# A selective scan in 128 steps: four state tiles and four decay tiles instead of five and three, and the experts' choice spread over the steps

## The chip, the cores and the metric

The kernel runs on one core of a Trainium2 chip. The time is the device time of one execution in microseconds (us). A core has five engines, each with its own queue that it works through in order: TensorE (PE in the profile; PEld are its weight loads), VectorE (DVE), ScalarE (ACT), GpSimd (POOL) and SyncE (SP), which here issues most of the DMA transfers. [...]

## What is computed

Two transformer layers on x of 4 x 256 tokens by 512. Layer 0 is an attention with low-rank latents beside a gated feed-forward; layer 1 is a Mamba block beside a mixture of LoRA experts. The part that matters here is layer 1:

```python
proj = hidden_states @ in_proj_w            # x, z = split; 1024 channels each
xc = silu(conv4(x) + conv_b)                # causal, 4 taps, per channel
ssm_p = einsum('bdl,ed->ble', xc, x_proj_w) # 32 for dt, 16 for B, 16 for C
dt_r, Bm, Cm = rmsnorm of the three parts
dt = softplus(dt_r @ dt_proj_w.T + dt_bias)
# for every t:  h = exp(dt*A)*h + dt*B*x ;  y = sum over 16 states of h*C
y = (ys + D_param * xc) * silu(z)
out = y @ out_proj_w.T
...
logits = x @ router_W.T                     # 8 experts
probs = softmax(logits); top 2, lowest index first on a tie
rw = top_vals / sum(top_vals)
inc = ((x @ lora_A) * w_dense) @ lora_B     # 16 ranks an expert
x = x + mamba + x @ base_W.T + inc * 2
```

## The kernel before, in words

Everything is laid out by hand: the order in the program is the order in each engine's queue. Layer 0 and the convolution of the first batch take the time up to about 327 us. Then come `total` = 128 steps, one for each batch b (4), block of 128 channels c (8) and group of four states g (4), so `u = 32*b + 4*c + g`; `PER` is 32 and `NU` 4. A tile of a step is 128 partitions by 4 x 256: 32 channels times four states on the partitions, four channel quarters and 256 tokens along the row.

One step u goes through the engines like this:

- `spread` (L937): SP copies `dt` and `dt*x` of a block c, which POOL made and `send` (L933) wrote to device memory, into the tiles `dts` and `dus` (two buffers each), four DMAs each.
- `decays` (L971): ACT makes `exp(dt*A)` in four activations, into one of the `decay` tiles. There are three, `decay[(u-4) % 3]`, and the loop calls `decays(u + 2)` at the start of step u, so ACT can be two steps ahead.
- `scan_in` (L986): DVE multiplies B (`brow`, in PSUM) and `dus` into `bx`, a tile in PSUM with one buffer. From step 8 on a no-op of DVE's stands in front of it and waits for what the scan will need: the decays of u, and `hc` of step u-2.
- `scan` (L998): one DVE instruction runs the recurrence along the row, `h <- decay, bx`; POOL multiplies `h` with C into a tile of its own, `hc`. `h` has two buffers, `hc` three. The first four steps use tiles that belong to others (`lent`, L961).
- `states_sum` (L1019): eight PE instructions add up the states of `hc` into `ysum` (PSUM, one buffer). Step u's sum is the last PE work of step u+1.
- `take_sum` (L1028) on ACT, `gate` (L1032) on POOL, `out_mm` (L1120) and `out_x` (L1124) make the output.

Between these stands the rest of the work, put at a step by hand: `put(b, s, f, ...)` (L1248) places a call at the start of step 32b+s, `put_mid` between `bx` and the scan, `put_late` behind the scan, `put_end` behind the sum. Within a step the order is: `take_sum`, `decays`, what `put` placed, `scan_in`, what `put_mid` placed, `scan`, `gate`, what `put_late` placed, `states_sum` of the step before, what `put_end` placed.

During a batch the next one is prepared: `norm_stats` to `norm_copy` (L718 to L748), `px_mm` (L754), `conv_in`, `conv_taps` (L765, L793), `conv_silu` (L821), then `pp_mm` (L829; the first half at the end of step 17, the second at 18), `pp_square` (L836, at 19: ACT `sq`, a PE product, ACT `rs` twice), `pp_norm` (L844, DVE `nrm`, between `bx` and scan of step 21), `step_in` (L865; PE, then ACT; 21 and 22), `step_exp` (L880, ACT, two halves at 23), `step_out` (L912, POOL, 24 to 29), `step_x` (L923). `pz_mm` (L945) and `gate_silu` (L953) make the gate; the latter loads another activation table and loads the old one back. Products that leave PE go through `psmm`, three buffers in PSUM for all of them.

The experts are chosen in batches 0 and 2, for two batches at once. `router` (L1039) makes logits and LoRA products of 128 tokens, PE then an ACT copy into one part of the tile `ml`; the four stand at steps 16, 17, 19 and 20. `route_exp` (L1066) stands at step 23: two DVE operations on 128 x 32 and the exponential on ACT. `route` (L1072) stands at step 25 ahead of `bx`: 16 small DVE operations in a row on a tile `w` that takes the place of `bx` in PSUM, and four products `mid` on 128 x 128. `expert_turn` (L1098), `dense` (L1108) and `expert_out` (L1115) use the result on PE.

Of the kernel before, what the change touches and what calls it, by code (L numbers as in the profile page):

```python
# [41 lines left out]
def block_kernel(  # L42
# [894 lines left out]
    def spread(n, b, c):  # L937
        t = w1.tile([P, NG, S], F32, tag=f"{n}s", name=f"{n}s", bufs=2)
        src = live[n, b, c // 2][c % 2].rearrange("(k j) t -> j k t", k=NG)
        for i in range(NG):  # L940
            nc.sync.dma_start(t[i * NB : (i + 1) * NB], src)
        live[n + "s", b, c] = t
# [10 lines left out]
    def gate_silu(b, *ps):  # L953
# [6 lines left out]

    lent = {  # L961
        "d": ("d", "w_in", "d", "w_in"), "h": ("w_in", "u", "e", "u"),
        "hc": ("w_in", "lw", "w_in", "lw"),
    }

# [5 lines left out]
    def decays(u):  # L971
        b, c, g = u // PER, u % PER // NU, u % NU
        if u >= len(lent["d"]):
            da = decay[(u - 4) % 3]
        elif lent["d"][u] == "d":
            da = decay[0]
        else:
            da = lend("d", u)
            nc.gpsimd.memset(da[:, :, 0:1], 0.0)
        live["da", u] = da  # L980
        for k in range(NG):
            made["da", u] = nc.scalar.activation(  # L982
                da[:, k, 1:], live["dts", b, c][:, k, 1:], AF.Exp, scale=aneg[:, c, k, g : g + 1]
            )

    def scan_in(u):  # L986
        b, c, g = u // PER, u % PER // NU, u % NU
        if u >= 8:
            i = nc.vector.engine_nop()
            for n in (("da", u), ("hc", u - 2)):  # L990
                tc.add_manual_dep(i.ins, made[n].ins.name, early, reason="the scan's waits")
        bx = psx.tile([P, NG, S], F32, tag="bx", name="bx")
        nc.vector.tensor_tensor(  # L993
            bx, brow[g // 2][:, g % 2, :].unsqueeze(1).to_broadcast([P, NG, S]), live["dus", b, c], ALU.mult
        )
        live["bx"] = bx

    def scan(u, parts=1):  # L998
        b, c, g = u // PER, u % PER // NU, u % NU
        da, bx = live.pop(("da", u)), live["bx"]  # L1000
        if u < len(lent["h"]):
            h, hc = lend("h", u), lend("hc", u)
        else:
            h = act.tile([P, NG, S], F32, tag="h", name="h", bufs=2)
            hc = act.tile([P, NG, S], F32, tag="hc", name="hc", bufs=3)
        for k in range(parts):
            n = slice(k * NG // parts, (k + 1) * NG // parts)
            nc.vector.tensor_tensor_scan(  # L1008
                h[:, n].rearrange("p n t -> p (n t)"), da[:, n].rearrange("p n t -> p (n t)"),
                bx[:, n].rearrange("p n t -> p (n t)"), 0.0, ALU.mult, ALU.add,  # L1010
            )

            made["hc", u] = (nc.vector if k == NG - 1 else nc.gpsimd).tensor_tensor(  # L1013
                hc[:, n], h[:, n],
                crows[b][:, g, :].unsqueeze(1).to_broadcast([P, NG // parts, S]), ALU.mult,
            )
        live["hc", u] = hc

    def states_sum(u):  # L1019
# [4 lines left out]
        for k in range(NG):  # L1024
            mm(ysum[k * NB : (k + 1) * NB, :], lhsT=stack, rhs=hc[:, k, :],  # L1025
               start=False, stop=(g == NU - 1))

# [20 lines left out]
    NR = 4  # L1048
    m1 = w1.tile([P, NR], F32, name="m1")
    b2 = w1.tile([P, NR], F32, name="b2")  # L1050
    ex = w1.tile([P, NR, NE], F32, name="ex")
    sel2 = w1.tile([P, NR, NE], F32, name="sel2")
    rev = cst[:, C_REV : C_REV + NE].unsqueeze(1).to_broadcast([P, NR, NE])
# [3 lines left out]

    def first_of(out, tmp, val, top):

        nc.vector.tensor_reduce(top, val, AX.X, ALU.max)  # L1060
        nc.vector.tensor_tensor(tmp, val, over(top), ALU.is_equal)
        nc.vector.tensor_tensor(tmp, tmp, rev, ALU.mult)
        nc.vector.tensor_reduce(m1, tmp, AX.X, ALU.max)
        nc.vector.tensor_tensor(out, tmp, over(m1), ALU.is_equal)

    def route_exp(b):  # L1066
        lg = live["ml"][:, :, 0:NE]
        nc.vector.tensor_reduce(m1, lg, AX.X, ALU.max)
        nc.vector.tensor_tensor(ex, lg, over(m1), ALU.subtract)
        nc.scalar.activation(ex, ex, AF.Exp)  # L1070

    def route(b):  # L1072

        w = psx.tile([P, NG, S], F32, tag="bx", name="w")
        m2 = w[:, 0, 0:NR]
        sel, best, tmp = (
            w[:, k, 0 : NR * NE].rearrange("p (i e) -> p i e", e=NE) for k in (1, 2, 3)
        )
        first_of(sel, sel, ex, m2)

        nc.vector.scalar_tensor_tensor(best, sel, -4.0, ex, ALU.mult, ALU.add)
        first_of(sel2, tmp, best, b2)
        nc.vector.tensor_tensor(sel, sel, sel2, ALU.add)
        nc.vector.tensor_tensor(sel, sel, ex, ALU.mult)
        nc.vector.tensor_tensor(m2, m2, b2, ALU.add)
        nc.vector.reciprocal(b2, m2)

        nc.vector.scalar_tensor_tensor(sel, sel, 2.0, over(b2), ALU.mult, ALU.mult)
        for n in range(2):
            mid = act.tile([P, 2, NE, LR], F32, tag="mid", name="mid", bufs=2)  # L1090
            for i in (2 * n, 2 * n + 1):
                nc.vector.tensor_tensor(
                    mid[:, i % 2], live["ml"][:, i, NE:].rearrange("p (e r) -> p e r", r=LR),
                    sel[:, i, :].unsqueeze(2).to_broadcast([P, NE, LR]), ALU.mult,
                )
            live["mid", b + n] = mid

# [129 lines left out]
    def open_act():  # L1227
        nonlocal act
        l0.close()
        act = ctx.enter_context(tc.tile_pool(name="act", bufs=1))  # L1230
        decay_tile(act)
        decay_tile(act)
        for n, shape, d in (("rl", [P, HC, NE + P], rl_d), ("bw", [P, HC, D], base_d),
# [29 lines left out]
    for b in range(B):  # L1263
# [59 lines left out]
        if nxt < B:  # L1323
# [21 lines left out]
            put(b, 22, c_rows, nxt, 0)  # L1345
            if b % 2 == 0:
                put(b, 23, route_exp, b)
            put(b, 23, step_exp, nxt, 0, slice(0, 2))
# [12 lines left out]
            put(b, 25, load_z, nxt, 1)  # L1361
            for k, u in enumerate((27, 28, 29, 31)):
                put(b, u, pz_mm, nxt, k // 2, k % 2)
            if b % 2 == 0:
                for i, u in enumerate((16, 17, 19, 20)):
                    put(b, u, router, b, i)
                put(b, 25, route, b)
            put(b, 26, expert_turn, b)
            put(b, 25, dense, b, 1, 0)
            put(b, 26, dense, b, 1, 1)  # L1370
            put(b, 28, expert_out, b, 1)
        else:
# [165 lines left out]
```

## Time and profile before

| | us |
|---|---|
| runs of the kernel before: median (lowest to highest, 3 runs) | 840.59 (839.35 to 841.75) |
| the profiled execution's own time | 840.18 |
| its span, from the first to the last instruction | 838.4 |
| granted TensorE clock, mean over the span | 0.953 |
| busy in the span: PE | 750.9 (90%) |
| DVE | 654.6 (78%) |
| ACT | 554.2 (66%) |
| POOL | 496.9 (59%) |
| PE busy from 345 to 832 us (487 us) | 421.7 |

Busy time is counted from an instruction's start to its end; waits, branches and the issue of DMAs are not counted. The shares are means over the whole span: DVE, at 78% in all, is busy for nine tenths and more of most slices after 430 us. A row of the groups names the line, the engine, what is written and read, how often, the busy time, the mean time of one in nanoseconds and, after the last bar, how long the engine had stood idle just before and what ended that. In a view in order of time each row has the start, the time taken, the engine and line, and in brackets the idle time before it.

### The profile page before, as it was taken

How to read it: one execution, taken by the hardware profiler on the slowest of the kernel's cores; microseconds unless marked ns; L12 is line 12 of the kernel's file. 1: busy time of each engine (PE TensorE's matmuls, PEld its weight loads, DVE VectorE, ACT ScalarE, POOL GpSimd, SP SyncE). 2: the span in 40 equal slices, each digit the busy share in tenths (PEclk: the TensorE clock that was granted, in tenths of full speed). 3: DMA queues.
4: the chain of work that ended last, by engine and by line, in shares of the span. 5: the costliest groups of instructions: out<-in, count | busy, mean ns of one | idle time of the engine just before them, and what ended most of it. 6: DMA issues, size and time to landing. Idle time of an engine off the chain costs nothing.

```text
span 838.4 us, 11286 instructions
## 1 busy us (share of the span) xinstructions
PE 750.9 (90%) x3846; PEld 429.6 (51%) x3846; DVE 654.6 (78%) x604; ACT 554.2 (66%) x1124; POOL 496.9 (59%) x389
## 2 busy tenths in 40 slices
PE   4999999999999999999887999897899987876985
PEld 2665545666555676666543456444457544322331
DVE  4486756288644535797899999988999999999996
ACT  4335564435556277699895898687898787865661
POOL 3133232001343333678878799769799769798775
PEclk9799999999999999999999899989999989988898
DMA  7233332001222322454593544433554443443400
GB/s 226 63 101 106 96 101 63 1 1 38 76 76 79 115 57 64 149 141 126 130 217 109 160 150 115 126 91 105 144 165 114 112 110 92 119 114 120 113 26 25
DMA packets 68644, 86.72 MB, mean 103 GB/s; under 512 B 12221, under 2 KB 52169, under 8 KB 68458
## 3 DMA queue, kind: packets, MB, share of 16 engines
q1 hardware_dynamic: 58794, 65.81, 29.0%
q0 software_dynamic: 9072, 18.35, 7.8%
q10 hardware_dynamic: 720, 1.84, 0.6%
q8 instruction: 30, 0.49, 0.3%
q14 instruction: 28, 0.23, 0.1%
HBM read 66.58 MB, written 10.22 MB: 92 GB/s over the span
## 4 chain that ended last, share of the span: by engine, by line
PE 45%; DVE 23%; POOL 12%; ACT 9%; issue 5%; DMA 5%; SPq 1%; POOLq 0%; ACTq 0%; DVEq 0%
DVE h L1008 11%; POOL hc L1013 8%; PE pg L444 6%; DVE bx L993 6%; PE pu L444 5%; PE po L469 5%; PE av L397 4%; ACT decay L982 3%; PE po L1121 2%; PE px L759 2%; DMA dus<-dud 2%; PE scT L386 2%; DVE mpl L354 2%; PE ysum L1025 2%; DMA dts<-dtd 2%
## 5 line engine op out<-in xcount | busy, mean ns | idle before, releaser
L1013 POOL TENSOR_TENSOR hc<-h,cr 128x1024 f32<-128x1024 f32 (+1 forms) x130 | 301.9, 2324 | 80.5 <-DVE h L1008 70.4
L1008 DVE TENSOR_TENSOR_SCAN h<-decay,bx 128x1024 f32<-128x1024 f32 (+1 forms) x129 | 288.1, 2235 | 8.5 <-PE po L469 3.6
L982 ACT ACTIVATE decay<-dts,aneg 128x255 f32<-128x255 f32 x504 | 213.6, 501 | 52.8 <-DVE h L1008 38.2
L993 DVE TENSOR_TENSOR bx<-brow,dus 128x1024 f32<-128x1024 f32 x128 | 157.7, 1232 | 24.2 <-ACT decay L982 9.3
L1025 PE MATMUL ysum<-hc,stack 128*32 128x256 f32 x1024 | 88.4, 417 | 39.3 <-POOL hc L1013 39.3
L456 POOL TENSOR_TENSOR hlo<-g,hhi 128x512 fp32r<-128x512 f32 x28 | 35.8, 1280 | 115.0 <-ACT hhi L455 115.0
L354 DVE TENSOR_REDUCE mpl<-sc 128x4 f32<-128x1024 f32 x64 | 76.7, 1220 | 22.8 <-PE sc L352 21.3
L427 POOL DMA_DIRECT2D wgu<-in_wgu x56 | 31.1, 555 | 96.0 <-PE pg L444 95.0
L388 ACT ACTIVATE pe<-scT 128x1024 f32<-128x1024 f32 x64 | 64.0, 1023 | 22.9 <-PE sc L352 14.3
L1121 PE MATMUL po<-ow,xc 128*128 128x512 f32 x128 | 72.4, 671 | 5.3 <-POOL xc L1033 4.9
L1025 PEld LDWEIGHTS ysum<-hc,stack 128*32 128x32 f32 x1024 | 21.2, 111 | 99.1 <-POOL hc L1013 69.7
L950 PE MATMUL pz<-xn1T,w_in 128*128 128x256 f32 x256 | 69.3, 419 | 0.0
L759 PE MATMUL px<-xn1T,w_in 128*128 128x256 f32 x256 | 61.0, 383 | 0.4 <-ACT sz L956 0.3
L950 PEld LDWEIGHTS pz<-xn1T,w_in 128*128 128x128 f32 x256 | 50.2, 205 | 19.8 <-issue 11.6
L759 PEld LDWEIGHTS px<-xn1T,w_in 128*128 128x128 f32 x256 | 47.5, 190 | 13.1 <-issue 3.1
L452 DVE SCALAR_TENSOR_TENSOR g<-g,pg 128x512 f32<-128x512 f32 x28 | 19.2, 687 | 43.0 <-ACT g L451 43.0
L444 PE MATMUL pg<-xhi,wgu 128*128 128x512 f32 x112 | 49.7, 443 | 1.0 <-ACT xhi L244 1.0
L469 PE MATMUL po<-wd,hhi 128*128 128x512 f32 x112 | 49.2, 439 | 0.0
L444 PE MATMUL pu<-xhi,wgu 128*128 128x512 f32 x112 | 47.5, 424 | 0.8 <-DVE g L454 0.8
L455 ACT CAST hhi<-g 128x512 fp32r<-128x512 f32 x28 | 17.3, 619 | 45.8 <-DVE g L454 45.8
L444 PE MATMUL pg<-xlo,wgu 128*128 128x512 f32 x112 | 44.9, 401 | 0.7 <-DVE xlo L251 0.7
L444 PE MATMUL pu<-xlo,wgu 128*128 128x512 f32 x112 | 44.6, 398 | 0.0
(237 smaller groups left out, 1276.8 us busy)
## 6 DMA issues: line engine op xcount, KB each, us to landing
dts<-dtd SPq DMA_DIRECT2D x124, 128.0 KB, 2.8
dus<-dud SPq DMA_DIRECT2D x124, 128.0 KB, 3.0
wgu<-in_wgu POOLq DMA_DIRECT2D x56, 256.0 KB, 2.7
w_in<-in_inz SPq DMA_DIRECT2D x16, 512.0 KB, 4.7
w_in<-in_inx SPq DMA_DIRECT2D x14, 512.0 KB, 4.4
dtd<-dt SPq DMA_DIRECT2D x15, 256.0 KB, 2.3
dud<-du SPq DMA_DIRECT2D x15, 256.0 KB, 2.3
wd<-in_wd POOLq DMA_DIRECT2D x7, 512.0 KB, 3.5
```

Source lines behind the costliest of these rows:

```text
L354: nc.vector.tensor_reduce(mpl2[b % 2][:, qb, 2 * hp : 2 * hp + 2, 16 + 2 * gq : 18 + 2 * gq], sc.rearrange("p i (f k) -> p i f k", f=2), A ...
L388: nc.scalar.activation(pes[b, k][:, 2 * t : 2 * t + 2, :], sc, AF.Exp)
L444: mm(ps, lhsT=wgus[i][:, hc, :], rhs=xs[j][:, hc, :], start=(hc == 0 and j == 0), stop=(hc == HC - 1 and j == 1))
L469: mm(po, lhsT=hids[th][j][:, m, i * P : (i + 1) * P], rhs=wd[:, m, :], start=False, stop=(m == MC - 1 and j == 1))
L759: mm(px[:, i, :], lhsT=w[:, i, hc, :], rhs=xns[b][:, hc, :], start=(hc == 0), stop=(hc == HC - 1))
L950: mm(pz[:, i, :], lhsT=w[:, i, hc, :], rhs=xns[b][:, hc, :], start=(hc == 0), stop=(hc == HC - 1))
L982: made["da", u] = nc.scalar.activation(da[:, k, 1:], live["dts", b, c][:, k, 1:], AF.Exp, scale=aneg[:, c, k, g : g + 1])
L993: nc.vector.tensor_tensor(bx, brow[g // 2][:, g % 2, :].unsqueeze(1).to_broadcast([P, NG, S]), live["dus", b, c], ALU.mult)
L1008: nc.vector.tensor_tensor_scan(h[:, n].rearrange("p n t -> p (n t)"), da[:, n].rearrange("p n t -> p (n t)"), bx[:, n].rearrange("p n t -> ...
L1013: made["hc", u] = (nc.vector if k == NG - 1 else nc.gpsimd).tensor_tensor(hc[:, n], h[:, n], crows[b][:, g, :].unsqueeze(1).to_broadcast([ ...
L1025: mm(ysum[k * NB : (k + 1) * NB, :], lhsT=stack, rhs=hc[:, k, :], start=False, stop=(g == NU - 1))
L1121: mm(live["po", b, i], lhsT=xcs[b][:, c, i * P : (i + 1) * P], rhs=late_w["ow"][:, c, :], start=False, stop=(c == DC - 1))
```

## The change

- `h` gets four buffers, and POOL multiplies with C in place; `hc` as a tile is gone (`lent` loses its third row, and step 1 takes `lw` instead of `u`).
- There are four decay tiles, and `decays(v)` is called at step v-3 (v-2 for the first step of a batch; 5 and 6 at step 3), where it was v-2.
- The no-op in front of `bx` waits for the decays of u, for the product with C of step u-4, for the sum of step u-4, and at the first step of a block for the four DMAs of `dus`.
- The choice works on the logits' difference from their maximum; only the second weight's exponential is taken (`e2`, two small activations on ACT). It is a generator of 15 DVE operations: operation 1 behind scan 20, 2 between `bx` and scan of 21, 3 behind scan 21, and so on to 15 behind scan 27. They work on tiles of their own in SBUF. The `mid` products go to POOL, one for each batch of the two, behind steps 27 and 28.
- The four `router` stand at 16, 17, 18 and 19. In batches 0 and 2, `dense`, `expert_turn` and `expert_out` stand three steps later, and one `pz_mm` at 31 instead of 29.

```diff
-        for i in range(NG):
-            nc.sync.dma_start(t[i * NB : (i + 1) * NB], src)
+        made[n, b, c] = [nc.sync.dma_start(t[i * NB : (i + 1) * NB], src) for i in range(NG)]
...
-    lent = {
-        "d": ("d", "w_in", "d", "w_in"), "h": ("w_in", "u", "e", "u"),
-        "hc": ("w_in", "lw", "w_in", "lw"),
-    }
+    lent = {"d": ("d", "w_in", "d", "w_in"), "h": ("w_in", "lw", "e", "u")}
+    ahead = 3
...
-            da = decay[(u - 4) % 3]
+            da = decay[(u - 4) % (ahead + 1)]
...
         if u >= 8:
             i = nc.vector.engine_nop()
-            for n in (("da", u), ("hc", u - 2)):
-                tc.add_manual_dep(i.ins, made[n].ins.name, early, reason="the scan's waits")
+            first = made["du", b, c] if g == 0 else []
+            for j in (*first, made["da", u], made["hc", u - 4], made["sum", u - 4]):
+                tc.add_manual_dep(i.ins, j.ins.name, early, reason="the scan's waits")
...
-            h = act.tile([P, NG, S], F32, tag="h", name="h", bufs=2)
-            hc = act.tile([P, NG, S], F32, tag="hc", name="hc", bufs=3)
+            h = act.tile([P, NG, S], F32, tag="h", name="h", bufs=4)
...
-                hc[:, n], h[:, n],
+                h[:, n], h[:, n],
...
+    def route():
+
+        vec_ = nc.vector
         lg = live["ml"][:, :, 0:NE]
+        vec_.tensor_reduce(m1, lg, AX.X, ALU.max)
+        yield
+        vec_.tensor_tensor(dl, lg, over(m1), ALU.subtract)
+        yield
+        vec_.scalar_tensor_tensor(sel1, dl, 0.0, rev, ALU.is_equal, ALU.mult)
+        yield
+        vec_.tensor_reduce(m1, sel1, AX.X, ALU.max)
+        yield
+        vec_.tensor_tensor(sel1, sel1, over(m1), ALU.is_equal)
+        yield
+
+        vec_.scalar_tensor_tensor(dl, sel1, -3e38, dl, ALU.mult, ALU.add)
+        yield
+        vec_.tensor_reduce(b2, dl, AX.X, ALU.max)
+        nc.scalar.activation(e2, b2, AF.Exp)
+        nc.scalar.activation(m1, e2, AF.Identity, bias=1.0)
+        yield
+        vec_.tensor_tensor(sel2, dl, over(b2), ALU.is_equal)
+        yield
+        vec_.tensor_tensor(sel2, sel2, rev, ALU.mult)
+        yield
+        vec_.tensor_reduce(b2, sel2, AX.X, ALU.max)
+        yield
+        vec_.tensor_tensor(sel2, sel2, over(b2), ALU.is_equal)
+        yield
+        vec_.reciprocal(m1, m1)
+        yield
+        vec_.tensor_tensor(sel2, sel2, over(e2), ALU.mult)
+        yield
+        vec_.tensor_tensor(sel1, sel1, sel2, ALU.add)
+        yield
+
+        vec_.scalar_tensor_tensor(sel1, sel1, 2.0, over(m1), ALU.mult, ALU.mult)
+        yield
+
+    def expert_mid(b, n):
+        mid = act.tile([P, 2, NE, LR], F32, tag="mid", name="mid", bufs=2)
+        i = slice(2 * n, 2 * n + 2)
+        nc.gpsimd.tensor_tensor(
+            mid, live["ml"][:, i, NE:].rearrange("p i (e r) -> p i e r", r=LR),
+            sel1[:, i, :].unsqueeze(3).to_broadcast([P, 2, NE, LR]), ALU.mult,
         )
+        live["mid", b + n] = mid
...
-            for k, u in enumerate((27, 28, 29, 31)):
+            for k, u in enumerate((27, 28, 29, 31) if b % 2 else (27, 28, 31, 31)):
                 put(b, u, pz_mm, nxt, k // 2, k % 2)
             if b % 2 == 0:
-                for i, u in enumerate((16, 17, 19, 20)):
+                for i, u in enumerate((16, 17, 18, 19)):
                     put(b, u, router, b, i)
-                put(b, 25, route, b)
-            put(b, 26, expert_turn, b)
-            put(b, 25, dense, b, 1, 0)
-            put(b, 26, dense, b, 1, 1)
-            put(b, 28, expert_out, b, 1)
+                choice = route()
+                for k in range(15):
+                    (put_late, put_mid)[k % 2](b, 20 + (k + 1) // 2, next, choice)
+                put_late(b, 27, expert_mid, b, 0)
+                put_late(b, 28, expert_mid, b, 1)
+            o = 3 if b % 2 == 0 else 0
+            put(b, 26 + o, expert_turn, b)
+            put(b, 25 + o, dense, b, 1, 0)
+            put(b, 26 + o, dense, b, 1, 1)
+            put(b, 28 + o, expert_out, b, 1)
...
+    due = {}
+    for v in range(5, total):
+        due.setdefault(max(v - ahead + (v % PER == 0), 3), []).append(v)
     for u in range(total + 2):
...
-        if 3 <= u < total - 2:
-            decays(u + 2)
+        for v in due.get(u, ()):
+            decays(v)
```

More of the change, by code (lines that the diff above doesn't have):

```diff
@@ L1001, in scan @@
         if u < len(lent["h"]):
[L1002 removed]
+            h = lend("h", u)
         else:
[L1004 to L1005 removed]
+            h = act.tile([P, NG, S], F32, tag="h", name="h", bufs=4)
         for k in range(parts):
@@ L1013, in scan @@
             made["hc", u] = (nc.vector if k == NG - 1 else nc.gpsimd).tensor_tensor(
-                hc[:, n], h[:, n],
+                h[:, n], h[:, n],
                 crows[b][:, g, :].unsqueeze(1).to_broadcast([P, NG // parts, S]), ALU.mult,
             )
-        live["hc", u] = hc
+        live["hc", u] = h
     def states_sum(u):
@@ L1024, in states_sum @@
         for k in range(NG):
-            mm(ysum[k * NB : (k + 1) * NB, :], lhsT=stack, rhs=hc[:, k, :],
-               start=False, stop=(g == NU - 1))
+            made["sum", u] = mm(ysum[k * NB : (k + 1) * NB, :], lhsT=stack, rhs=hc[:, k, :],
+                                start=False, stop=(g == NU - 1))
     def take_sum(b, c):
@@ L1048, in block_kernel @@
     NR = 4
[L1049 to L1052, printed above, removed]
+    m1, b2, e2 = (w1.tile([P, NR], F32, name=n) for n in ("m1", "b2", "e2"))
+    dl, sel1, sel2 = (w1.tile([P, NR, NE], F32, name=n) for n in ("dl", "sel1", "sel2"))
     rev = cst[:, C_REV : C_REV + NE].unsqueeze(1).to_broadcast([P, NR, NE])
@@ L1056, in over @@
         return v.unsqueeze(2).to_broadcast([P, NR, NE])
[L1058 to L1066, printed above, removed]
-        lg = live["ml"][:, :, 0:NE]
-        nc.vector.tensor_reduce(m1, lg, AX.X, ALU.max)
-        nc.vector.tensor_tensor(ex, lg, over(m1), ALU.subtract)
-        nc.scalar.activation(ex, ex, AF.Exp)
@@ L1072, in route @@
[L1072 to L1077, printed above, removed]
-        )
[L1079 to L1096, printed above, removed]
+    def route():
+        vec_ = nc.vector
+        lg = live["ml"][:, :, 0:NE]
+        vec_.tensor_reduce(m1, lg, AX.X, ALU.max)
[30 more added lines that the diff above has]
+        yield
@@ L1230, in open_act @@
         act = ctx.enter_context(tc.tile_pool(name="act", bufs=1))
-        decay_tile(act)
-        decay_tile(act)
+        for _ in range(ahead):
+            decay_tile(act)
         for n, shape, d in (("rl", [P, HC, NE + P], rl_d), ("bw", [P, HC, D], base_d),
@@ L1345, in block_kernel @@
             put(b, 22, c_rows, nxt, 0)
-            if b % 2 == 0:
-                put(b, 23, route_exp, b)
             put(b, 23, step_exp, nxt, 0, slice(0, 2))
```

## The prediction

> **What bounds the kernel now.** I read the groups first, then who waited for whom, then the order in time of DVE, ACT and PE around each wait. Up to 327 us the feed-forward and attention stages run, which the change doesn't touch. From 327 to 830 us come 128 steps: step u is the u-th `bx` and the u-th `h` (counted from 0), batch b is steps 32b to 32b+31.
>
> ```profile
> L1008 DVE TENSOR_TENSOR_SCAN h<-decay,bx 128x1024 f32<-128x1024 f32 (+1 forms) x129 | 288.1, 2235 | 8.5 <-PE po L469 3.6
> L982 ACT ACTIVATE decay<-dts,aneg 128x255 f32<-128x255 f32 x504 | 213.6, 501 | 52.8 <-DVE h L1008 38.2
> L993 DVE TENSOR_TENSOR bx<-brow,dus 128x1024 f32<-128x1024 f32 x128 | 157.7, 1232 | 24.2 <-ACT decay L982 9.3
> ```
>
> An undisturbed step starts its scan 1.27 us after its `bx`, and the next `bx` 2.32 us after that: 3.59 us, DVE's own work. 128 of them are 460 of the 503 us; the rest is small work and waits. The waits of `bx` are these (the view of line 993):
>
> ```profile
>   ACT decay L982: 9.3, 8
>   POOL hc L1013: 6.7, 10
>   ACT pad L771: 3.2, 1
> ```
>
> The 3.2 us (step 16) I count to POOL: `hc` of step 14 ended 0.2 us before that `bx`. So 19 us are what four tiles can remove at most. But DVE isn't alone. In each batch PE and ACT make the next batch's convolution, then `pp`, `sq`, `rs`, and DVE's `nrm` (step 21) needs `rs`. From 349.9 to 403 us ACT has 0.2 us of idle time, and from 362 to 408 PE has 1.8, all of it waiting for ACT: a wait that DVE loses there comes back at the end of that chain. This is ACT at that end, in batch 0 (start, length, line):
>
> ```profile
> 413.59 0.27 ACT L1046 COPY ml<-pr 128x136 f32<-128x136 f32 x1
> 413.76 3.29 ACT L982 ACTIVATE decay<-dts,aneg 128x255 f32<-128x255 f32 x8
> 417.25 0.38 ACT L839 ACTIVATE sq<-pp 64x256 f32<-64x256 f32 x1 [0.20 <-PE pp L833]
> 418.39 0.47 ACT L714 ACTIVATE rs<-pp,eps 64x256 f32<-64x256 f32 x1 [0.76 <-PE pp L840]
> 418.89 0.42 ACT L715 ACTIVATE rs<-rs 64x256 f32<-64x256 f32 x1
> 419.51 0.27 ACT L1046 COPY ml<-pr 128x136 f32<-128x136 f32 x1 [0.21 <-PE pr L1044]
> ```
>
> ACT fills the wait for `pp` with two steps' decays, and `ml` comes after `rs`.
>
> **The parts.** *State tiles.* `bx` waits for `hc` of step u-4 instead of u-2; that ended 7.2 us or more before every `bx`, so all ten waits on POOL go. Late next is `ysum` of step u-4 (PE), which DVE now waits for itself: it ended 0.64 us before `bx` at step 53, 1.6 at 21, 1.8 at 57, 2.2 at 85, over 2.7 elsewhere. Multiplying in place costs POOL nothing (L918, in place, 1.27 us; L927, not in place, 1.27). The extra wait of the no-op is checked under the 2.29 us scan: steps with one and with more semaphore checks both take 3.59. I take 0; were a 0.05 us check exposed at each, 6 us.
>
> *Decay tiles.* ACT computes each step's decays one step (3.59 us) earlier; its gate, the scan that frees the tile, is the same number of instructions back. Where ACT has idle time ahead of a burst, the lead is real; where it has none, everything behind comes 1.6 us later. The largest wait, step 58:
>
> ```profile
> 557.23 1.70 ACT L982 ACTIVATE decay<-dts,aneg 128x255 f32<-128x255 f32 x4
> ...
> 565.33 1.70 ACT L982 ACTIVATE decay<-dts,aneg 128x255 f32<-128x255 f32 x4
> ...
> 567.16 1.23 DVE L993 TENSOR_TENSOR bx<-brow,dus 128x1024 f32<-128x1024 f32 x1 [4.12 <-ACT decay L982]
> ```
>
> Between the two groups lie eight activations of `step_exp`. The second slot now makes step 59, whose `bx` stood at 570.75.
>
> *The choice.* Removed from DVE: at step 25 `bx` started at 438.80 instead of 434.17, at 89 5.36 us late (0.83 of it a wait for `ex`), and 0.2 at each `route_exp`: 10.4 in all. Added: 15 small operations, each alone, twice. The trace has neighbours: `sh` (0.13 us) ahead of a `bx` delayed it 0.07; `nrm` (0.47) between `bx` and scan delayed that 0.26; in the old chain each operation took 0.23. Nearest to a lone 0.2 us operation are the first two: 0.1, with 0.05 and 0.23 as ends: 3.0 us (1.5 to 6.9). Four `mid` products go to POOL as two (0.72 each by the 128x256 row of L1033): POOL then lags some 3 us at steps 27 to 31, covered by the four tiles; without that cover DVE would wait the 3 us.
>
> [...]
>
> *The new waits of the choice.* They are what I weigh most. `router` 2 moves from step 19 to 18, behind the second half of `pp` on PE, and its `ml` copy stands on ACT ahead of the decays of step 22 and of `sq`. `sq` thus waits for `router` and a decay group, and the first of the 15 (after scan 20) reads all four `ml`, the last of which is behind `rs`. Behind it on DVE stand `bx` 21, `nrm` and everything later.
>
> **The sum, by batch** (against the trace).
> Batch 0: decays 5, 6 and 7 now precede the table load at 353.18; no idle time absorbs it: +1.5 along the chain (bounds 0, 1.7), `pp` ends 417.2 + 1.5 = 418.7. Then `router` 1.2, copy 0.3, decays 1.7, `sq` 0.4, its product 0.7, `rs` 0.95 (`router` 3 runs beside it), `ml` 0.3, hand-overs 0.3: 424.5; `bx` 21 at 424.7, not 419.38: +5.3. All that DVE saved up to there (8.6) is lost in this wait. Steps 21 to 25 took 19.42; now 4 x 3.59 + 0.27 + 8 x 0.1 = 15.4: -4.0. Six more operations +0.6, the `hc` wait of step 29 -0.8. Together +1.1.
> Batch 1: `dense`, `expert_turn`, `expert_out` and one `pz` of batch 0 move to steps 28 to 31, 4.4 us more PE work in 14; PE's 6 us of idle there take most of it, but step 31 has 6 us, so `step_in` comes 1.3 late, of which 0.8 is absorbed at 507 (PE waited for `hc`). `bx` 59 follows its decays: 567.03 + 0.13 + 0.5 = 567.7, not 570.75: -3.1. The `hc` wait of step 61: -0.8. Together -3.9 (bounds -5.1, -0.8).
> Batch 2: `pp` ended 665.7; the same row of `router` to `ml` gives `bx` 85 at 671.4, not 668.50: +2.9. Steps 85 to 89: 20.15 becomes 15.4: -4.7. The tenth operation (between `bx` and scan 89) overwrites `b2`, which ACT's `e2` reads, and `e2` stands behind `step_exp`, by the rows of 681 to 690 at 690.0; DVE is there at 688.1: +1.9 (bounds 0, 4). In batch 0 this wait just misses (440.9 against 441.3). Six operations +0.6, `hc` at 93 -0.8. Together -0.1.
> Batch 3: the wait at 102 and trifles -0.5.
> Other parts at 0: the early lent tiles (`u` is free after `ysum` 3 at 354.3, wanted at 359.4; if not, ACT stands until then), the third memset (0.1).
> In all -3.4: span 838.4 - 3.4 = 835.0, with the 1.8 around it (840.18 - 838.4) 836.8. The runs shown have a median 0.4 above the profiled one, so **837** for the median.
>
> **Rivals.** *A: the chain's end doesn't hold DVE* (`ml` is there in time). For it: in the trace `ml` 3 came at 421.5, DVE read it at 426.7. Then only `rs` holds: batch 0 +0.4 -4.0 +0.6 -0.8 = -3.8, batch 2 -0.7 -4.7 +0.6 -0.8 = -5.6, batches 1 and 3 as above: 840.2 - 13.8, about 827. Against it: the order of the queues.
> *B, slower: PE's clock falls in the new wait.* Place: from `pp` to `ml` 3 PE has only `router`, `ysum`, a product and `router`, with 1.7 us pauses. Before, after 3.9 us of idle, the 16 `pp` took 5.35 where batch 2's took 3.9, and the stretch 405 to 420 has a granted clock of 0.89. If those four (1.2 + 0.65 + 0.65 + 1.2) take double, each choice costs 3.7 more: 844. It decides from some 2.7 us each. Against it: the row for 656 to 690 stayed at 0.90 through similar pauses.
> *C: it doesn't do what it says.* ACT's lead is gone at step 59 because PE's moved work makes `step_in` late by all the 3.1 us: 840, no change. For it: PE is 90% busy; against it: its idle time at 445 to 466.
>
> **Chances.** Forecast 0.48, A 0.22, B 0.18, C 0.12. Measurement tells 0.3% (2.5 us) from no change. The forecast's own range, 834 to 840, splits 0.28 faster, 0.19 same, 0.01 slower; A is faster; B slower; C 0.10 same, 0.02 slower. So 0.50, 0.29, 0.21. Range 828 to 844: B's time, and A's nearer part.
>
> **What would show it.** DVE idle 8 to 11 us after scan 20 and 3 to 5 after scan 84, ended by ACT's `ml`; `sq` behind a decay group; some 2 us ahead of the tenth operation in batch 2; no wait of `bx` on `hc`; the 4.1 us wait at step 58 under 1; steps with one small operation at 3.6 to 3.8. I am wrong if `bx` 21 comes before 422 us, if small operations cost over 0.2 each, or if waits on `ysum` add up to over 2 us.

## The result and the profile after

The changed kernel takes **846.52 us** (median of 6 runs, 845.34 to 848.07) against 840.66 for the kernel before (6 runs, 839.35 to 842.55): ratio 1.0066, 95% interval 1.0051 to 1.0081. The forecast was 837 with a range of 828 to 844, so it was wrong in sign, and the time lies outside the range. The profiled execution took 848.07 us, span 846.1.

These are the three large groups of the page of the changed kernel (busy us, mean ns of one, idle time ahead and its releasers):

```profile
L1005 DVE TENSOR_TENSOR_SCAN h<-decay,bx 128x1024 f32<-128x1024 f32 (+1 forms) x129 | 288.0, 2235 | 8.1 <-PE po L469 3.6
L979 ACT ACTIVATE decay<-dts,aneg 128x255 f32<-128x255 f32 x504 | 212.3, 501 | 43.0 <-DVE h L1005 28.0
L991 DVE TENSOR_TENSOR bx<-brow,dus 128x1024 f32<-128x1024 f32 x128 | 157.6, 1232 | 19.1 <-DMA dus<-dud 6.8
```

DVE's large instructions are what they were (2235 and 1232 ns each). What `bx` waits for (the view of line 991) has changed:

```profile
  DMA dus<-dud: 6.8, 5
  PE ysum L1022: 6.2, 5
  ACT decay L979: 2.1, 2
```

No wait of `bx` on POOL is left, and ACT's decays fell from 9.3 to 2.1, as the tiles were to do; but DMAs and PE's sums now end last: 13.0 us, where ACT's decays and POOL had 16.0. And among the waits by pair (us, times, longest) there is a new one:

```profile
DVE m L1057 <- ACT ml L1043: 11.9, 2, 6.3
```

That is the first operation of the choice, in both batches. ACT's order around it in batch 0 is the one that the prediction wrote down:

```profile
417.19 1.70 ACT L979 ACTIVATE decay<-dts,aneg 128x255 f32<-128x255 f32 x4
421.79 0.27 ACT L1043 COPY ml<-pr 128x136 f32<-128x136 f32 x1 [2.90 <-PE pr L1041]
421.96 1.70 ACT L979 ACTIVATE decay<-dts,aneg 128x255 f32<-128x255 f32 x4
423.56 0.36 ACT L839 ACTIVATE sq<-pp 64x256 f32<-64x256 f32 x1
424.66 0.47 ACT L714 ACTIVATE rs<-pp,eps 64x256 f32<-64x256 f32 x1 [0.73 <-PE pp L840]
425.16 0.42 ACT L715 ACTIVATE rs<-rs 64x256 f32<-64x256 f32 x1
425.78 0.27 ACT L1043 COPY ml<-pr 128x136 f32<-128x136 f32 x1 [0.20 <-PE pr L1041]
```

`sq` stands behind `ml` of router 2 and a decay group, the last `ml` behind `rs`; `bx` 21 started at 426.20 (forecast 424.7). What the prediction had not seen is in DVE's order in time, steps 23 to 25:

```profile
433.61 0.17 DVE L1065 TENSOR_TENSOR sel<-sel,m 128x32 f32<-128x32 f32 x1
433.73 1.23 DVE L991 TENSOR_TENSOR bx<-brow,dus 128x1024 f32<-128x1024 f32 x1
434.87 1.39 DVE L1068 SCALAR_TENSOR_TENSOR dl<-sel,dl 128x32 f32<-128x32 f32 x1
...
439.63 1.40 DVE L1074 TENSOR_TENSOR sel<-dl,b 128x32 f32<-128x32 f32 x1
...
443.15 0.16 DVE L1076 TENSOR_TENSOR sel<-sel,cst 128x32 f32<-128x32 f32 x1
443.26 1.23 DVE L991 TENSOR_TENSOR bx<-brow,dus 128x1024 f32<-128x1024 f32 x1
444.40 0.17 DVE L1078 TENSOR_REDUCE b<-sel 128x4 f32<-128x32 f32 x1
```

Two operations on 128 x 32 elements take 1.4 us, others of the same size 0.17. The same stretch of POOL:

```profile
433.86 2.35 POOL L1010 TENSOR_TENSOR h<-h,cr 128x1024 f32<-128x1024 f32 x1 [1.23 <-DVE sel L1065]
...
438.62 2.36 POOL L1010 TENSOR_TENSOR h<-h,cr 128x1024 f32<-128x1024 f32 x1 [1.73 <-DVE b L1070]
```

The long ones begin while POOL multiplies, and end 0.05 us after it (436.26 and 436.21, 441.03 and 440.98). The operations 6, 8, 14 and 15 are stretched like this, in both batches: 1.39, 1.40, 1.33 and 1.02 us in the mean (15 stands behind a scan, and what POOL does then is the product `du<-dt,xc`).

Against the trace of before (start of the same `bx`), the changed kernel is 5.8 us late at step 32, 3.4 at 64, 8.3 at 96 and 7.8 at 127. By batch: +5.8, -2.4, +4.9, -0.5, where the forecast had +1.1, -3.9, -0.1, -0.5.

### The profile page after: what moved, and what is told of

It reads as the page before. It is cut to its first block, busy times and chain, and to the rows that moved or that the text cites. A ratio compares the mean times of both kernels' runs of the same rounds, so it can differ in the third digit from the quotient of the medians.

```text
span 846.1 us, 11262 instructions
## 1 busy us (share of the span) xinstructions
PE 755.6 (89%) x3846; PEld 435.1 (51%) x3846; DVE 656.3 (78%) x590; ACT 554.4 (66%) x1126; POOL 499.3 (59%) x394
## 4 chain that ended last, share of the span: by engine, by line
PE 52%; DVE 21%; ACT 12%; POOL 6%; issue 5%; DMA 3%; SPq 1%; ACTq 0%; DVEq 0%; POOLq 0%
DVE h L1005 9%; PE pg L444 6%; PE px L759 6%; DVE bx L991 6%; PE pu L444 5%; PE av L397 4%; PE px L806 4%; POOL h L1010 4%; PE ysum L1022 4%; ACT decay L979 3%; PE po L469 3%; PE po L1124 3%; PE pz L949 3%; PE scT L386 2%; DVE mpl L354 2%
## 5 line engine op out<-in xcount | busy, mean ns | idle before, releaser
L1010 POOL TENSOR_TENSOR h<-h,cr 128x1024 f32<-128x1024 f32 (+1 forms) x130 | 302.0, 2328 | 79.5 <-DVE h L1005 51.2
L1005 DVE TENSOR_TENSOR_SCAN h<-decay,bx 128x1024 f32<-128x1024 f32 (+1 forms) x129 | 288.0, 2235 | 8.1 <-PE po L469 3.6
L991 DVE TENSOR_TENSOR bx<-brow,dus 128x1024 f32<-128x1024 f32 x128 | 157.6, 1232 | 19.1 <-DMA dus<-dud 6.8
L1022 PE MATMUL ysum<-h,stack 128*32 128x256 f32 x1024 | 89.1, 424 | 35.2 <-POOL h L1010 35.2
L949 PE MATMUL pz<-xn1T,w_in 128*128 128x256 f32 x256 | 73.4, 439 | 0.0
L1124 PE MATMUL po<-ow,xc 128*128 128x512 f32 x128 | 70.1, 657 | 0.4 <-DVE xc L1414 0.4
L1022 PEld LDWEIGHTS ysum<-h,stack 128*32 128x32 f32 x1024 | 21.5, 112 | 95.1 <-POOL h L1010 58.7
L949 PEld LDWEIGHTS pz<-xn1T,w_in 128*128 128x128 f32 x256 | 54.0, 220 | 21.3 <-issue 11.2
L759 PE MATMUL px<-xn1T,w_in 128*128 128x256 f32 x256 | 63.1, 393 | 0.4 <-ACT sz L955 0.3
L759 PEld LDWEIGHTS px<-xn1T,w_in 128*128 128x128 f32 x256 | 49.2, 196 | 14.6 <-issue 4.4
```

The costliest lines, as they stand in the source:

```text
L759: mm(px[:, i, :], lhsT=w[:, i, hc, :], rhs=xns[b][:, hc, :], start=(hc == 0), stop=(hc == HC - 1))
L949: mm(pz[:, i, :], lhsT=w[:, i, hc, :], rhs=xns[b][:, hc, :], start=(hc == 0), stop=(hc == HC - 1))
L991: nc.vector.tensor_tensor(bx, brow[g // 2][:, g % 2, :].unsqueeze(1).to_broadcast([P, NG, S]), live["dus", b, c], ALU.mult)
L1005: nc.vector.tensor_tensor_scan(h[:, n].rearrange("p n t -> p (n t)"), da[:, n].rearrange("p n t -> p (n t)"), bx[:, n].rearrange("p n t -> ...
L1022: made["sum", u] = mm(ysum[k * NB : (k + 1) * NB, :], lhsT=stack, rhs=hc[:, k, :], start=False, stop=(g == NU - 1))
L1124: mm(live["po", b, i], lhsT=xcs[b][:, c, i * P : (i + 1) * P], rhs=late_w["ow"][:, c, :], start=False, stop=(c == DC - 1))
```

## The experiments

Times are medians, with the ratio to the kernel before on the same chip and its 95% interval; a time without a ratio is that of a single run. The kernel before stood between 840.3 and 841.2 us in these comparisons.

**Which operations are stretched.** Line 1104 has two SBUF tiles as inputs, 1106 a tile and a broadcast one, 1108 a PSUM and an SBUF tile, 1112 one tile. Each is put into steps of batch 3 of the kernel before:

```diff
+    put_late(3, 6, probe, "init")
+    for s in range(4):
+        put_mid(3, 8 + s, probe, "two")
+        put_mid(3, 12 + s, probe, "psum")
+        put_mid(3, 16 + s, probe, "one")
+        put_late(3, 20 + s, probe, "two")
+    for s in range(2):
+        put_mid(3, 25 + s, probe, "over")
+        for _ in range(2):
+            put_late(3, 27 + s, probe, "two")
```

> The kernel before, with extra small VectorE operations in batch 3, whose results nothing uses (128x32 or 128x4, in the choice's tiles): in steps 8 to 11, between the input product and the scan, one with two SBUF tensors; steps 12 to 15, same place, one with a PSUM and an SBUF tensor; 16 to 19, same place, a reduction of one SBUF tensor; 20 to 23, right behind the scan, one with two SBUF tensors; 25 and 26, between product and scan, an SBUF tensor and a broadcast 128x4 SBUF tile; 27 and 28, right behind the scan, two with two SBUF tensors each. Theory L (an operation with two SBUF tensor inputs that is issued while POOL multiplies two SBUF tensors waits until POOL is done): steps 8 to 11 and 25, 26 have operations of 1.0 to 1.4 us that end with POOL's product, steps of 4.6 to 4.8; steps 12 to 19 operations of 0.15 to 0.3 and steps of 3.6 to 3.7; steps 20 to 23 operations of 0.2, steps of 3.6 to 3.8; in 27 and 28 the first of the two takes 0.2 and the second 2.0 to 2.4. Rival N (the place between product and scan is dear for any operation): steps 8 to 19 and 25, 26 all 4.6 to 4.8. Rival D (the dependence on an operation just before is what took the time): all 0.2 and 3.6 to 3.8, the second of each pair some 0.1 more.

Its lines' durations (ns: least, median, most):

```profile
L1104 DVE TENSOR_TENSOR sel<-ex,sel x12: 165/178/1612, 745.1 to 827.0; 128x32 f32<-128x32 f32 x12
L1106 DVE TENSOR_TENSOR sel<-ex,b x2: 1391/1397/1403, 811.0 to 815.8; 128x32 f32<-128x32 f32 x2
L1108 DVE TENSOR_TENSOR sel<-brow,ex x4: 178/180/180, 764.3 to 775.0; 128x32 f32<-128x32 f32 x4
L1112 DVE TENSOR_REDUCE m<-ex x4: 174/174/175, 778.7 to 789.5; 128x4 f32<-128x32 f32 x4
```

Between product and scan the ones with two SBUF inputs made steps of 4.74 to 4.99 us (the 1.37 to 1.61 of them end with POOL's product); with a PSUM input, or a single one, the step stayed at 3.59 (one at 3.67), and so did a step with a lone two-input operation right behind the scan, ahead of POOL's product. So theory L, but for the pairs: both of a pair began before POOL did, and cost 0.36 and 0.20 us for the two. For the six stretched operations the trace names nothing that DVE waited for, and no idle time ahead of them; they ended 0.04 to 0.05 us behind POOL's product all the same. The run took 848.07 us, 7.9 of it the longer steps. A lone small operation that isn't stretched costs DVE nothing that can be read, not 0.1.

**Take the stretch away.** All two-input operations of the changed kernel get one input from PSUM, with values that are not those of the choice, so the experts' weights are not computed:

```diff
+        alt = brow[0][:, 0, 0 : NR * NE].rearrange("p (i e) -> p i e", e=NE)
-        vec_.tensor_tensor(sel2, dl, over(b2), ALU.is_equal)
+        vec_.tensor_tensor(sel2, dl, alt, ALU.is_equal)
...
```

> The changed kernel with its ten two-input operations of the choice in the same places and order, but in each the second (or first) input is a 128x32 slice of the input rows in PSUM instead of an SBUF tile; the experts' weights are therefore not computed. Theory L (two SBUF inputs wait for POOL): no small operation over 0.3 us; batch 0 and batch 2 shorter by the four stretched operations of each (1.39 + 1.40 + 1.37 + 1.02 us, less 0.2 each): 846.5 - 8.7 = 838, up to 842 if batch 1 takes back what batch 0 gains. Rival N (place or number of operations): 845 to 848.

847.55 us, ratio 1.0076 (1.0053 to 1.0098): no gain. The stretch is gone, and this came in its place (DVE, batch 0):

```profile
438.39 0.18 DVE L1075 TENSOR_TENSOR sel<-dl,brow 128x32 f32<-128x32 f32 x1
...
444.29 0.19 DVE L1079 TENSOR_REDUCE b<-sel 128x4 f32<-128x32 f32 x1 [2.23 <-ACT e L1072]
```

The tenth operation overwrites `b2`, which ACT still has to read for `e2`; the stretched operations had covered that wait. It is 2.23 us in batch 0 and 3.47 in batch 2 (none and 1.10 in the changed kernel). From `bx` 22 to `bx` 28 the changed kernel took 25.97 us, this one 23.81; of the 2.2 us gained, 1.4 went ahead of `bx` 39 in a wait for ACT's decays, 0.6 ahead of `bx` 50 in one for PE's sum, and at step 64 it was 0.1 ahead. L's mechanism was right, what it expected the removal to be worth was not.

**All at once.** No two SBUF inputs (the weights are again left out), `b` of the tenth operation written elsewhere, routers and first operation later:

```diff
-        vec_.tensor_reduce(b2, sel2, AX.X, ALU.max)
+        vec_.tensor_reduce(dl[:, :, 0], sel2, AX.X, ALU.max)
-                for i, u in enumerate((16, 17, 18, 19)):
+                for i, u in enumerate((16, 17, 19, 20)):
-                    (put_late, put_mid)[k % 2](b, 20 + (k + 1) // 2, next, choice)
+                    (put_late, put_mid)[k % 2 or not k](b, max(20 + (k + 1) // 2, 21), next, choice)
```

> The changed kernel with three things taken away together: each two-input operation of the choice has one input from PSUM (the experts' weights are therefore not computed), the tenth operation writes into dl and so no longer waits for ACT's e2, and the routers are back at steps 16, 17, 19, 20 with the first operation behind nrm in step 21. Theory S (these three are the choice's whole loss; one alone gains little, since the next wait takes its place): no operation over 0.3 us, no wait for e2, a wait for ml of 0 to 2.5 us; 846.5 - 8.7 - 4 = 834 (831 to 837), the time of the tiles alone or less. Rival B (PE at half clock and the chain from batch to batch hold DVE, whatever it saves in the choice): 841 to 846, with new waits of bx on ACT's decays and PE's ysum in batches 1 to 3 of as much as the three took.

841.28 us, ratio 1.0008 (0.9992 to 1.0023). From `bx` 22 to 28 it took 21.52 us, six bare steps of 3.59, with twelve operations among them, as in batch 2 (21.57). So these twelve operations are free in their steps, as S said; but the kernel is 7 us from S's 834 and inside B's range. The first operation still waits for `ml`, within what S allowed (us, times, longest):

```profile
DVE m L1058 <- ACT ml L1043: 4.3, 2, 2.6
```

The rest of DVE's lead is taken back by waits outside the choice: 2.0 us for decays ahead of `bx` 39, 2.9 for `dus` ahead of `bx` 96, 1.5 for decays ahead of `bx` 103 in the profiled run (835.86 us, the fastest of twelve). A second profile:

> The changed kernel without the three causes, again (the experts' weights are not computed), for another profile. Theory G: 841 to 842 and a clock of 0.947, the 5 to 6 us against the earlier profile lost at waits on ACT or PE in batches 1 to 3, with half-clock stretches of 7 us or more before them. Rival H: lost ahead of step 10, or everywhere a little.

840.40 us with a clock of 0.947 (0.953 in the first profile): against the first it lost 1.2 us ahead of the steps, 1.3 at steps 10 to 12, 2.3 at steps 74 to 84 behind a half-clock stretch at 616 us that the first doesn't have, 1.3 at 84, and won 1.3 back at steps 97 and 102. That is theory G for batch 2, where the time goes in waits on PE, ACT and a DMA; but that stretch is 3.4 us long, not 7, and 2.5 us came ahead of the steps and at their start.

**Each part of it alone.** The routers back and the first operation between `bx` and scan 21, with the rest as changed (the last two edits above):

> The changed kernel with the four router products back at steps 16, 17, 19, 20 and the first of the fifteen operations moved from behind scan 20 to behind the input product of step 21, after nrm. Theory M (the new order costs ahead of sq a router product and a decay group, and the last ml behind rs, together 3 to 4 us per choice): no wait for ml over 1 us, sq right behind pp; 846.5 - 6 to 8 = 839.5 (838 to 841). Rival A (without ml nothing holds DVE there: the whole waits of 5.6 and 6.3 go): 835. Rival C (the end of the chain, pp to rs, holds DVE as long): 845 to 847.

845.36 us, ratio 1.0061 (1.0040 to 1.0082); the wait for `ml` is 1.75 and 2.55 us, with `sq` right behind `pp`. The traces differ by 3.5 us at the end, the medians by 1.2; less than M said. From this kernel to the one with all three the stretch and the wait for `e2` alone are taken away: steps 22 to 27 and 86 to 91 are 9.7 us shorter in the profiles, the time 4.1 us (medians; 4.5 by the ratios). So less than half of what DVE wins in these steps reaches the end.

**The choice's slots.** Two-input operations alone behind a scan, one-input ones between, the last three on POOL; and the same with the routers back:

```diff
+                for place, s in ((put_late, 20), (put_late, 21), (put_late, 22), (put_mid, 23),
+                                 (put_late, 23), (put_late, 24), (put_mid, 25), (put_late, 25),
+                                 (put_late, 26), (put_mid, 27), (put_late, 27)):
+                    place(b, s, next, choice)
```

> The changed kernel, its choice still beginning behind scan 20 and ending behind scan 27, but seven operations with two SBUF tensors each stand alone right behind a scan, the operations with one input between product and scan (or, the reciprocal, behind the reduction), and the last three two-input operations go to POOL. Theory L: the operations of 1.0 to 1.4 us, some 4.5 us per choice, go, DVE's small operations are 0.15 to 0.3 each: 846.5 - 8 to 9 = 838 (836 to 840). Rival N or D: 844 to 847, with some operations still over 1 us. Both: the wait for ml behind scan 20 and scan 84 stays at 5 to 7 us each.

846.29 us, ratio 1.0047 (1.0026 to 1.0067).

> As slots, but the four router products are back at steps 16, 17, 19, 20 and the first reduction is between product and scan of step 21, behind nrm. Theory M (the new order of the routers and the early first operation cost what the waits of 5.6 and 6.3 us show, less what the end of the pp, sq, rs chain would take anyway): bx 21 3 to 5 us earlier than in slots, bx 85 4 to 6 earlier, no wait for ml over 1 us: 838 - 9 = 829 (827 to 833). Rival C (the chain from pp to rs holds DVE there anyway, whatever the routers do): 836 to 838.

842.31 us, ratio 1.0010 (0.9992 to 1.0029). The first missed: some operations behind a scan were stretched all the same (1.25 us at step 24, 0.76 at step 27 of batch 0), which I put down to the other products that POOL has there, by operation 15 of the changed kernel (1.02 us beside `du`); and `e2` was waited for (0.84 us in batch 0). The second gained 4.0 us on it, less than half of what M said.

**The parts on the tiles' side.** The four state and decay tiles alone, with the choice, the routers and PE's products as before; later once more; and the new choice alone on the old tiles:

> The kernel before with the four state tiles and the four decay tiles and their waits alone; the choice, the routers and the experts' products as before. Theory T (the tiles do what the prediction's sum gave them: +1.5 to +3 at the end of the chain of batch 0, -0.8 each at steps 29, 61, 93, -3 at step 59, -0.5 in batch 3): 838 (836 to 840). Rival W (the tiles bring the loss: decays three steps ahead delay ACT's chain in every batch, and ysum's release becomes a wait): 842 to 847.

835.84 us, ratio 0.9939 (0.9918 to 0.9960).

> The four state and decay tiles with the old choice, again. If their 835.8 holds without luck: 835 to 837, every run of a granted clock of 0.950 or more. If PE's half-clock stretches fall by chance: single runs up to 841, with a clock under 0.948.

835.91 us, ratio 0.9941 (0.9920 to 0.9962); single runs from 830.85 to 839.10.

> The kernel before with the new choice alone (operations, routers, experts' products), with five tiles for states and products and three decay tiles. Theory L and M (what the choice costs doesn't depend on the tiles): its stretched operations 4.4 per choice, its wait for ml 3 to 4, less the 4.8 and 5.6 removed: 841 + 6 = 847 (844 to 852). If tiles and choice only add up, the difference of the changed kernel and of the tiles alone, 10.7: 851. Rival: the loss comes from the two together (the tiles' new waits let the choice's waits through): 840 to 842.

850.45 us, ratio 1.0117 (1.0090 to 1.0144). The tiles win some 5 us, and the choice loses 9.6 on the old tiles and 10.4 (5.9 + 4.5) on the new ones: tiles and choice add up. Two pieces of the choice by themselves on the tiles alone:

```diff
-                for i, u in enumerate((16, 17, 19, 20)):
+                for i, u in enumerate((16, 17, 18, 19)):
```

> The four state and decay tiles with the old choice, and the router products of batches 0 and 2 at steps 16, 17, 18, 19. Theory Q (sq comes 2.9 us later behind a router product and a decay group, and nrm and scan 21 and 85 wait for it): 835.8 + 2 to 5 = 839.5 (838 to 841). Rival (the old choice gives the time back, since it then waits less for ex and rs): 835 to 837.

841.41 us, ratio 1.0006 (0.9993 to 1.0020): +5.5 on the tiles alone. ACT, batch 0, first with this order, then in the tiles alone:

```profile
421.58 0.27 ACT L1043 COPY ml<-pr 128x136 f32<-128x136 f32 x1 [2.89 <-PE pr L1041]
421.75 1.70 ACT L979 ACTIVATE decay<-dts,aneg 128x255 f32<-128x255 f32 x4
423.35 0.37 ACT L839 ACTIVATE sq<-pp 64x256 f32<-64x256 f32 x1
```

```profile
413.41 3.29 ACT L979 ACTIVATE decay<-dts,aneg 128x255 f32<-128x255 f32 x8
416.90 0.38 ACT L839 ACTIVATE sq<-pp 64x256 f32<-64x256 f32 x1 [0.19 <-PE pp L833]
```

With the old order ACT runs two decay groups while `pp` is made, and `sq` is ready at its end; with the new one ACT stands 2.9 us for a router product that PE makes behind `pp`, and the second decay group comes after that, ahead of `sq`.

```diff
-            for k, u in enumerate((27, 28, 29, 31)):
+            for k, u in enumerate((27, 28, 29, 31) if b % 2 else (27, 28, 31, 31)):
+            o = 3 if b % 2 == 0 else 0
-            put(b, 26, expert_turn, b)
+            put(b, 26 + o, expert_turn, b)
...
```

> The four state and decay tiles with the old choice, and the PE products of the experts (dense, expert_turn, expert_out, one pz) of batches 0 and 2 in steps 28 to 31 in place of 25 to 28, as in the changed kernel. Theory E (the moved products leave PE idle at steps 25 to 27, so that its clock halves, and hold up step_in and what follows): 835.8 + 3 to 5 = 839.5 (838 to 841), with a wait of bx on ACT's decays at step 38 or 39 of 1 to 2 us. Rival (PE's idle time takes them in, as the prediction had it for all but 0.5 us): 835 to 837.

840.45 us, ratio 0.9992 (0.9970 to 1.0014): +4.5. The profiled run was one of two in ten near 836, so this is a second profile:

> The tiles with the experts' PE products moved, again, for another profile. Theory G (the executions at 839 to 842 are those in which a wait of PE between steps 25 and 53 leaves it at half clock for 7 to 10 us instead of 3.4, and ACT's decays, the pp, sq, rs chain or ysum then come late): a mean clock of 0.947 or less, and against the earlier profile 3 to 6 us lost at waits of bx on ACT or PE in batch 1 or behind it. Rival H (the time is lost ahead of the steps, or everywhere a little): the steps agree within 1 us from step 10 to the end. At 836 and 0.954 the run says nothing.

841.33 us, clock 0.943. PE's wait at step 26, first in the tiles alone, then here:

```profile
438.11 0.70 PE L1020 MATMUL ysum<-xc,dgs 128*128 128x256 f32 x2 [3.72 <-ACT xc L1027]
```

```profile
439.59 1.22 PE L1020 MATMUL ysum<-xc,dgs 128*128 128x256 f32 x2 [5.64 <-ACT xc L1027]
...
444.86 1.08 PE L1022 MATMUL ysum<-h,stack 128*32 128x256 f32 x8 [3.04 <-POOL h L1010]
```

With nothing of the experts to do, PE stands 5.64 and 3.04 us, and its clock is at half for 13.65 us there (3.41 in the tiles alone). The profile of 836.05 has the same two waits (5.63 and 3.04) and 10.24 us of half clock. And the time isn't lost at those steps: against that profile this one lost 1.7 us from step 9 to 32, 2.3 between steps 74 and 96 and 1.5 at step 102. Half of G: the clock is lower, the place isn't the one that I named.

**The clock at the start.** Decays 5 to 12 two steps ahead again, and, apart from that, 24 more transposes ahead of `pt`:

```diff
-        due.setdefault(max(v - ahead + (v % PER == 0), 3), []).append(v)
+        due.setdefault(max(v - (ahead if v > 12 else 2) + (v % PER == 0), 3), []).append(v)
```

> The changed kernel, but the decays of steps 5 to 12 are computed two steps ahead as before; from step 13 on three ahead. Theory K (in the first steps the early decays hold up ACT's xnt, PE idles 3.5 instead of 1.9 us ahead of pt, and its clock stays at 0.50 for 10 us instead of 3.4): PE idle ahead of pt 1.9 us, half clock from 357 us for 3.4 us or none, the chain of batch 0 (pp) starts 3 us earlier, bx 21 at 422.5 to 423.5, 846.5 - 3 = 843.5 (842 to 845). Rival P (the length of the half clock is a matter of phase alone, not of the idle time): between 844 and 848, with half-clock stretches of 7 us or more still there in some runs. Rival T2 (the decays at the start are without effect): 846.5.

848.21 us, ratio 1.0085 (1.0063 to 1.0107); two of nine runs at 843.3 and 843.7 with a clock of 0.947, the others from 847.7 with 0.941 or less.

> The changed kernel with 24 transposes more, whose results are overwritten, in batch 0 ahead of pt: PE has work in the 3.5 us in which it waits for ACT's xnt. Theory K (that idle time is what brings the half clock from 357 us on): none or 3.4 us of half clock at 355 to 368 in place of 10 us, pp of batch 0 starts at 412 instead of 415.3, 846.5 - 3 = 843.5 (842 to 845). Rival P (the half clock comes by phase, whatever PE does there): 845 to 848 and half clock still there.

845.27 us, ratio 1.0057 (1.0034 to 1.0080). In the two profiled runs (843.28 and 845.27) PE waited 1.93 and 0.75 us ahead of `pt` in place of 3.52, and the half clock there lasted 3.4 us in place of 10.2; but neither makes the kernel reliably faster. K isn't borne out, P not excluded.

**Better than both.** The tiles alone, with the four `mid` products as two on POOL, and with the early decays as before as well:

> The four state and decay tiles with the old choice in PSUM at step 25, and only the four mid products (0.28 us each) moved from DVE to POOL, as two. Theory: steps 25 and 89 start 1.1 us earlier each: 835.8 - 2 = 834 (833 to 835.5). Rival (the chain's end or the later products of POOL take it back): 835.5 to 838.

835.90 us, ratio 0.9951 (0.9931 to 0.9971).

> As tiles_mid, but the decays of steps 5 to 12 two steps ahead, as before. Theory K (xnt and the chain of batch 0 come 1.6 us earlier, the half clock is shorter): 832.5 (831 to 834). Rival (the end of that chain doesn't hold DVE here, or phase decides): as tiles_mid, within 1 us.

836.30 us, ratio 0.9943 (0.9925 to 0.9961). Step 24 fell from 8.22 to 7.29 us with the `mid` products gone, step 88 stayed at 9.7 (DVE's wait for `ex` there grew from 1.57 to 2.51), and the time didn't move: the rival that the chain takes it back. Nothing tried is faster than the tiles alone, at 835.9.

## Why the prediction was wrong

I sort the sum's terms by part. Measured are differences of medians, each good to some 2 us; the last row is what is left of +5.9.

| part | forecast | measured |
|---|---|---|
| four tiles (+1.5 - 0.8 in batch 0, -4.4, -0.8, -0.5) | -5.0 | -4.5 and -5.4 |
| routers and early first operation (3.8 + 2.9) | +6.7 | +5.5 |
| experts' products moved on PE (the 0.5 at step 59) | +0.5 | +4.5 |
| operations in, old block out (-4.0 + 0.6, -4.7 + 1.9 + 0.6) | -5.6 | +0.3 |

These parts don't simply add: the routers cost 5.5 us on the tiles alone, and putting routers and first operation back in the changed kernel gave 1.2. So the last row is a remainder, not a measurement. By place, in the trace of the changed kernel against that of before, with the forecast in brackets: up to `bx` 21 +6.8 (+5.3), from there to step 32 -1.0 (-4.2), batch 1 -2.4 (-3.9), up to `bx` 85 +5.7 (+2.9), from there to step 96 -0.8 (-3.0), batch 3 -0.5 (-0.5). Half of the error lies in the steps of the choice.

*The tiles: right in the main.* No wait of `bx` on POOL is left, and the wait at step 58 is gone: `bx` 57 was 7.0 us late against before, `bx` 58 2.9. Yet "waits on `ysum` add up to over 2 us" was on my list of what makes me wrong, and they are 6.2, most of it at steps 17 and 53: the sums that are waited for there ended 3.4 and 7.0 us later than in the trace that I had read the slack from, and `bx` was less late than they. The 6.8 us for `dus`, 3.9 of them at step 20, stand in no term either.

*The new wait for `ml`: right in mechanism and order, but the chain ahead of it came later than the sum had it.* DVE stood 5.62 and 6.31 us ahead of the first operation, where 8 to 11 and 3 to 5 were forecast. From the end of `pp` to `bx` 21, and to `bx` 85, it took 5.57 us (forecast 6.0 and 5.7). But in batch 0 `pp` ended 3.4 us late, not 1.5: ACT's `xnt`, and with it PE's `pt`, came 1.7 later behind the early decays, as worked out, and PE's clock there was at half for 10.2 us. In batch 2 `pp` ended at 671.98, 6.3 us late, of which step 64 brought 3.4; the sum had nothing for the other 2.9, and no run shows what they are.

*The price of a small operation: the step that failed.* "0.1, with 0.05 and 0.23 as ends" was read from neighbours that met no such wait: `nrm` has an input in PSUM, and `sh`, with two in SBUF, ran while POOL did nothing (at 473.44 and 598.23 us). In the old block the work tile lay in PSUM; the change moved it to SBUF, and put half of the operations between product and scan, where POOL multiplies. Eight of the thirty took 1.02 to 1.40 us. The steps with them are 8.6 us longer than 3.59 (4.3 a choice), the other operations cost some 0.4 together, the wait for `e2` 1.1: that is 10.1, and the 10.4 us of the old block are spent. The forecast of 1.9 for that wait in batch 2 met 1.10, since DVE came late by the stretch; with the stretch gone it is 3.47.

What the runs show of this price: the two-input operations beside POOL's product took 1.02 to 1.40 us in the changed kernel and 1.37 to 1.61 in the probe, with their ends 0.04 to 0.05 us behind POOL's; and the eighth operation, 1.40 us long in the changed kernel, took 0.18 in its place in `one_input`, with one input from PSUM. By what POOL's product holds them isn't shown.

*Gains that were added up and don't add up.* The right price alone would not have made the forecast true. With all three causes gone, steps 21 to 31 are 3.3 us shorter than before in both profiles (forecast 4.2), and the median is still 841.28. Batch 1, for which the sum has -3.9 whatever batch 0 has won, then gains nothing (+0.3 and +0.2 us), while it gains 3.7 with the tiles alone and 1.6 to 1.7 where the experts' products are moved too. What DVE wins in one batch, waits for ACT and PE in the next take back.

*The experts' products: the other mis-sized term.* "PE's 6 us of idle there take most of it" counted PE's busy time, not what the gap left behind would do: with the same choice, the same routers and the same tiles the move alone costs 4.5 us. That the mean clock falls (0.943 in the median of ten runs, 0.951 in the ten of the tiles alone) is shown; the way from there to the lost time is only half seen.

*The rivals.* A, that `ml` is there in time, was plainly wrong. B had the sign, and with 844 came nearest, but not by its own reason: between `pp` and `ml` 3 the two router products took 1.19 us each, at full clock (a mean of 0.99 from 419 to 429 us). The stretches at half clock were longer elsewhere; that they turned the sign isn't shown. PE's clock, ahead of and behind `pt`, kernel before and then the changed one (columns: stretch, length, busy us of the engines, then PE's clock, DMA share, GB/s):

```profile
355.00:362.00 7.00, 4.98 (x24) 2.62 (x22) 6.71 (x4) 6.97 (x15) 3.63 (x2) 0.76 0.34 119
362.00:369.00 7.00, 7.00 (x43) 5.12 (x43) 6.85 (x4) 6.93 (x15) 5.04 (x4) 1.00 0.86 211
```

```profile
355.00:362.00 7.00, 3.48 (x16) 2.33 (x19) 6.80 (x4) 6.96 (x12) 3.59 (x3) 0.70 0.64 171
362.00:369.00 7.00, 7.00 (x32) 3.79 (x28) 6.76 (x5) 7.00 (x17) 5.05 (x4) 0.57 0.42 115
```

C, that ACT's lead would be gone at step 59, was wrong: `bx` 57 was 7.0 us late and `bx` 59 3.3.

*What stays open.* Why the same wait of PE is followed by 3.4 us of half clock in one execution and 10.2 in another; whether the moved products lose their 4.5 us by it alone; and why the changed kernel's `one_input` form gains nothing in the median although its steps are shorter. That last one I put down to the waits behind it (`e2`, decays, `ml`), which is shown only in part: the removal of all three gave 5.2 of the 10.7 us between the changed kernel and the tiles alone.

## What to carry to other kernels

Ahead of moving small VectorE operations, list for each where its tensors lie and what POOL does at that moment: with one input in PSUM, or a single one, they were free between two large instructions (steps of 3.59 us in the probe), and with two in SBUF beside a POOL product they took 1.0 to 1.6 us in place of 0.17. A change of several parts is best tried part by part, since here a gain of 5 us lay under a loss of 10. And a stall that is taken away is worth only what the next one behind it leaves: look for that wait (`e2` here) ahead of counting the gain.

## What the hardware showed

PE's clock was at half in stretches of 3.41, 6.83, 10.24 or 13.65 us, one to four times 3.41, in every profile that was read in half microseconds (the last stretch apart, which the end cuts off). Waits of PE of one length were followed by it or not: in the changed kernel half clock began between 620.5 and 621 us behind a wait of 1.62 us up to 619.15, and the same wait in the tiles alone, 1.59 us up to 609.55, was followed by none. The total at half clock from 327 us to the end of the span was 65 us in the kernel before, 66 in the tiles alone and 86 in the changed kernel. One kernel's runs differ by up to 8 us with it: the tiles alone took 839.1 at a mean clock of 0.942 and 830.85 at 0.964.
